# A message-passing layer on one core: tiles of 125 edges, the resident columns copied by VectorE instead of ScalarE, and silu made by ScalarE

## The chip, the cores and the metric

The kernel runs on one core of one Trainium2 chip. The time is device microseconds of one execution; the time before is the median of three runs. A profile is one more execution, taken with the hardware profiler; its own time and its span stand in the table below. Engines are named as in the profile: PE is TensorE, PEld its weight loads, DVE is VectorE, ACT is ScalarE, POOL is GpSimd, SP is SyncE. L513 is line 513 of the kernel before.

## The reference

12500 nodes have 64 features, 412500 edges 32 features each, sorted by receiver. All is float32.

```python
h = maximum(layernorm(x), 0)
msg_in = concatenate([h[src], h[dst], edge_attr], -1)          # 412500 x 160
messages = silu(msg_in @ W1 + b1) @ W2 + b2                    # 64 wide
att = softmax(silu(msg_in @ Wa1 + ba1) @ Wa2 + ba2, axis=0)    # over all edges
agg = segment_sum(messages * att, dst, 12500)
out = x + silu(concatenate([h, agg], -1) @ Wu1 + bu1) @ Wu2 + bu2
```

## The kernel before

**Node stage** (L132 to L279). Nodes lie 98 to a partition. The layer norm is made in chunks; hT, the transposed h, stays in SBUF (64 features of a node in one half of the partitions, so two nodes share a column). Two tables go to DRAM, each 128 floats a node: ts_d is h times the sender's part of Wa1 and W1 (`senders`, L226), tr_d the receiver's part with the bias (L267 to L278). The weights are halved beforehand (L248), so that the sum of an edge is half of the pre-activation.

**Edge loop** (`one_pass`, L360). Edges are taken in tiles of EP = 128, eight tiles (K) to a group: 403 groups (NG). The loop at L718 runs over the groups; every engine's program order is fixed by `pin`, so the order of the calls is the order of the work:

- `load(g+2)` (L504): eight indirect DMAs of GpSimd (L513), one for each tile, each fetching 128 rows of 512 bytes of ts_d, by the senders' numbers, into a tile gs of a pool with 7 buffers. SP fetches the window of tr_d that the group's receivers lie in (wins, L534), the edges' features (eo) and the receivers' numbers (dbs) for four groups at a time. DVE makes the one-hot rows of the receivers (L538). PE multiplies: one-hot and edge features by window and edge weights, into the PSUM tile pe (L542).
- Every second group from group 8 on is *chosen*: its last tile isn't gathered. Instead ScalarE copies one column of hT for each of its 128 edges, four bytes on each partition, at an address in a register (`columns`, L483). The registers are loaded 32 at a time (L479), in four bursts that are spread over two groups (`burst`, L486, SLOTS). DVE zeroes the half of the column that belongs to the other node (L547) and PE multiplies by the sender's weights (L548).
- `begin(g)` (L550): DVE adds gathered rows and PSUM into gs (L553; a chosen tile is copied, L555); ScalarE takes the tanh (L556).
- `end(g)` (L558): DVE makes silu from tanh, (tanh + 1) times the half sum, for the messages (L566, into acts) and for the attention (L572), multiplies by Wa2 (L574) and sums to one logit an edge (L577).
- Batches of four groups share a running maximum: `top` (L585), `weigh` (L599), which takes exp on ScalarE (L610) after the maximum over partitions.
- `sum_up` for a group some five earlier: `by_node` (L614) makes on DVE, with eight operations of 40 elements (L620), matrices that hold an edge's weight in its receiver's column; PE sums the messages with them (L626); ScalarE copies the result (L632), PE projects it (L637), and `put` (L640) adds it to the resident sums (L651, L655) and notes the maximum that they stand for (L658).

**Tail** (L789 on): the sums are rescaled, and the update of the nodes is made in 13 tiles.

If a receiver lies outside its window, a general path (L285) is run instead; it isn't with these inputs.

Of the kernel before, what the change touches and what calls it, by code (L numbers as in the profile page):

```python
# [19 lines left out]
EP = 128  # L20
# [37 lines left out]
def gnn_kernel(ctx: ExitStack, tc: tile.TileContext, n_edges, x, src, src_row, dst, dst_row, first, edge,  # L58
# [73 lines left out]
    with tc.tile_pool(name="node1", bufs=1) as node1, \  # L132
# [3 lines left out]

        sizes = [8] + [min(CB, NB - 16 - c) for c in range(0, NB - 16, CB)] + [8] if NB > 16 else [NB]
# [38 lines left out]
        pin(nc.scalar.activation(node1.tile([P, 1], F32, name="spare"), eps, AF.Sqrt))  # L176
        xms, sqs, rstds, hs, tss = ({} for _ in range(5))
# [5 lines left out]
        def subtract(i):  # L183

            n = chunks[i][1]
            total = node.tile([P, CB], F32, name="total")[:, :n]
            pin(nc.vector.tensor_reduce(total, xcs[i], AX.X, ALU.add))
            xm = xms[i] = node.tile([P, CB, D], F32, name="xm", bufs=3)[:, :n, :]
            pin(nc.vector.scalar_tensor_tensor(xm, total[:, :, None].to_broadcast([P, n, D]), -1.0 / D,
                                               xcs[i], op0=ALU.mult, op1=ALU.add))  # L190

        def square(i):
            n = chunks[i][1]
            sq = sqs[i] = node.tile([P, CB, D], F32, name="sq", bufs=3)[:, :n, :]
            pin(nc.scalar.activation(sq, xms[i], AF.Square))

        def totals(i):
            n = chunks[i][1]
            rstd = rstds[i] = node.tile([P, CB], F32, name="rstd")[:, :n]
            pin(nc.vector.tensor_reduce(rstd, sqs.pop(i), AX.X, ALU.add))  # L200
# [4 lines left out]
        def normal(i):  # L205
            n = chunks[i][1]
            rstd = rstds.pop(i)
            pin(nc.vector.reciprocal(rstd, rstd))
# [35 lines left out]
        nch = len(chunks)  # L244
# [22 lines left out]
        for c, nn in chunks:  # L267
# [9 lines left out]
            pin(nc.sync.dma_start(  # L277
                tr_d[:NP, :].rearrange("(p b) f -> p b f", b=NB)[:, c:c + nn, :], tr))  # L278
        pin(nc.sync.dma_start(tr_d[NP:, :], zero[:WR, :]))  # L279
# [80 lines left out]
def one_pass(tc, n_edges, v):  # L360
# [17 lines left out]
    with ExitStack() as ctx:  # L378
# [43 lines left out]
        with tc.tile_pool(name="work2", bufs=2) as work2, \  # L422
                tc.tile_pool(name="small", bufs=3) as small, \
                tc.tile_pool(name="pre_ps", bufs=AHEAD + 1, space=PSUM) as pre_ps, \
                tc.tile_pool(name="one_ps", bufs=1, space=PSUM) as one_ps:
            pes, gss, lgs, ps_, psums, sps, pps, ees, mts, nums, cols = ({} for _ in range(11))
# [12 lines left out]
            chosen = {g: i for i, g in enumerate(picks)}  # L439
            hT8 = v["hT"].rearrange("d b p -> d (b p)").bitcast(U8)  # L440
            sets = [(i, min(P, len(picks) - i)) for i in range(0, len(picks), P)]
# [3 lines left out]
            def places():  # L445
# [4 lines left out]
                for k, (i, n) in enumerate(sets):  # L450
                    e = (picks[i] * K + K - 1) * EP
                    nc.sync.dma_start(num[:n, k, :], bass.AP(
                        tensor=v["src_row"].tensor, offset=v["src_row"][:, e:].offset,
                        ap=[[EVERY * K * EP, n], [1, EP]]))
# [8 lines left out]
                for k, (i, n) in enumerate(sets):  # L463
                    nc.sync.dma_start(par_d[k * P:k * P + n, :], low[:n, k, :])
# [3 lines left out]
            def numbers(g):  # L468
                if g in chosen:
                    n = nums[g] = small.tile([P, EP], I32, name="half", bufs=3)  # L470
                    row = par_d[chosen[g]:chosen[g] + 1, :]
                    nc.sync.dma_start(n, bass.AP(tensor=row.tensor, offset=row.offset, ap=[[0, P], [1, EP]]))
                    cols[g] = small.tile([P, EP], F32, name="cols", bufs=3)

            def columns(g, first, n):
                if g not in chosen:
                    return
                to, i = cols[g].bitcast(U8), chosen[g]
                _, regs = nc.values_load_multi_w_load_instructions(  # L479
                    spots[i % P:i % P + 1, i // P, first:first + n], engines=[ENG.Activation],  # L480
                    min_val=HT_AT, max_val=HT_AT + 2 * NP - 4, skip_runtime_bounds_check_because=WHY)
                for i in range(n):
                    pin(nc.scalar.copy(to[:, 4 * (first + i):4 * (first + i) + 4],  # L483
                                       hT8[:, bass.ds(regs[i] - HT_AT, 4)]))

            def burst(g, k):  # L486
# [6 lines left out]
            tr_w = bass.AP(tensor=tr_d.tensor, offset=tr_d.offset,  # L493
                           ap=[[C, NP + WR - SHIFT], [SHIFT * C, 2], [1, C]])

            def registers(g, engine, at, base=base_sb, top=NP - 1):
                n = min(NQ, NG + (base is not base_sb) - g)
# [6 lines left out]
            def load(g):  # L504

                t = g * K
                if g % NQ == 0:
                    registers(g, ENG.SP, at_sp)
                full = gather.tile([P, K, C], F32, name="gs")
                gs = gss[g] = full[:EP]  # L510
                for j in range(K - (g in chosen)):
# [21 lines left out]
                for r in range(2):  # L533
                    nc.sync.dma_start(win[r * R:(r + 1) * R, :, r, :],  # L534
                                      tr_w[bass.ds(at_sp[g], R), :, :])
# [14 lines left out]
            def begin(g):  # L550

                n = K - (g in chosen)
                pin(nc.vector.tensor_tensor(gss[g][:, :n, :], pes[g][:, :n, :], gss[g][:, :n, :], ALU.add))  # L553
                if n < K:
                    pin(nc.vector.tensor_copy(gss[g][:, n, :], pes[g][:, n, :]))  # L555
                pin(nc.scalar.activation(pes[g], gss[g], AF.Tanh))  # L556

            def end(g, then=None):  # L558

                s = batch[g]  # L560
                if g == starts[s]:
                    lgs[s] = small.tile([EP, B * K], F32, name="lg")
                gs, th = gss.pop(g), pes.pop(g)

                def message():
                    pin(nc.vector.scalar_tensor_tensor(acts[g % ACTS][:, :, 0:U], th[:, :, U:C], 1.0,  # L566
                                                       gs[:, :, U:C], op0=ALU.add, op1=ALU.mult))

                if g < NG - 1:
                    message()  # L570
                att = th[:, :, 0:U]
                pin(nc.vector.scalar_tensor_tensor(att, th[:, :, 0:U], 1.0, gs[:, :, 0:U],  # L572
                                                   op0=ALU.add, op1=ALU.mult))
# [3 lines left out]
                pin(nc.vector.tensor_reduce(lgs[s][:, k:k + K], att, AX.X, ALU.add))  # L577
# [4 lines left out]
                if g == NG - 1:  # L582
                    message()

            def top(s):  # L585

                n = size[s] * K
                lg = lgs[s]
# [10 lines left out]
            def weigh(s):  # L599
# [5 lines left out]
                fall = small.tile([P, 1], F32, name="fall")  # L605
                pin(nc.vector.tensor_tensor(fall, nmax[:, s + 1:s + 2], nmax[:, s:s + 1], ALU.subtract))
                pin(nc.scalar.activation(scale[:, s:s + 1], fall, AF.Exp))
                p = ps_[s] = small.tile([EP, B * K], F32, name="p")
                psum = small.tile([EP, 1], F32, name="psum")
                pin(nc.scalar.activation(p[:, :n], lgs.pop(s)[:, :n], AF.Exp, bias=nmax[:EP, s + 1:s + 2],  # L610
                                         accum_out=psum))
                psums[s] = psum

            def by_node(g):  # L614
# [4 lines left out]
                for j in range(K):  # L619
                    pin(nc.vector.tensor_scalar(wt[:, j, :], iota_w[:EP, j // H, :],  # L620
                                                dloc[:, g * K + j:g * K + j + 1],
                                                p[:, k + j:k + j + 1],
                                                op0=ALU.is_equal, op1=ALU.mult))
# [94 lines left out]
            for g in range(NG):  # L718
# [6 lines left out]
                begin(g)  # L725
                if more and g < NG - 1:
# [10 lines left out]
                if g + AHEAD < NG:  # L737
                    load(g + AHEAD)
                numbers(g + 6)
# [384 lines left out]
```

## Time and profile before

| | |
|---|---|
| median of 3 runs | 3902.49 us (3900.42 to 3908.46) |
| profiled execution | 3904.89 us, span 3903.1 us |
| granted TensorE clock, mean | 0.642 |
| instructions | 72226 |
| indirect DMAs of POOL | 3032, busy 2871.4 us |
| column copies of ACT | 24576, busy 2415.5 us |
| DMA traffic | 391.30 MB, mean 100 GB/s |

How to read it: the page gives each engine's busy time, then groups of instructions by line, engine, operation and tile: busy time in all, mean length of one, then the engine's idle time before them and what ended it. "issue" is idle time that ended with nothing the profile shows, such as work of the engine's own sequencer. A time line gives start, length and, in brackets, the idle time ahead. Lengths of instructions that follow each other closely overlap, so what one takes of its engine is the distance of two starts.

### The profile page before, as it was taken

The page shows a single profiled execution, that of the slowest core. Times are in us where ns is not written, and L with a number is a line of the kernel's source. Part 1 is how long each engine was busy: PE and PEld are TensorE (multiplying, and loading weights), DVE is VectorE, ACT ScalarE, POOL GpSimd, SP SyncE. Part 2 cuts the span into 40 slices and gives each one's busy share as a digit, 9 for nine tenths or more (in the row PEclk, how much of TensorE's full clock was granted, in tenths as well). Part 3 has the DMA queues.
Part 4 walks back from the last instruction along what each step waited for, and adds up shares of the span by engine and source line. Part 5 has one row for each costly group of instructions (what it writes and reads, how often), then busy time and mean ns, then how long its engine had stood idle before and what let it go on. Part 6 is the DMA issues. An engine that isn't in the chain of part 4 may idle for free. (4 is left out here: it accounts for less than half of the span.)

```text
span 3903.1 us, 72226 instructions
## 1 busy us (share of the span) xinstructions
PE 2368.6 (61%) x11368; PEld 1927.2 (49%) x11368; DVE 3115.4 (80%) x8929; ACT 2954.1 (76%) x25797; POOL 2888.6 (74%) x3057
## 2 busy tenths in 40 slices
PE   6566656666666666665665656556565565555655
PEld 5454444454445554554444545445444454444545
DVE  6888787878788888887877877778777777877887
ACT  2887777777778888887877777878877878878712
POOL 3777777777777777777777777777777777777774
PEclk8766566666666657666666666666666666666666
DMA  7433334333433333333333333333333333333343
GB/s 280 114 104 94 102 100 106 94 104 99 107 93 97 97 97 91 94 97 94 87 97 85 97 93 89 97 86 97 93 88 97 86 96 91 90 97 86 95 116 86
DMA packets 228304, 391.30 MB, mean 100 GB/s; under 512 B 72369, under 2 KB 155762, under 8 KB 214770
## 3 DMA queue, kind: packets, MB, share of 16 engines
q0 software_dynamic: 97024, 198.90, 19.5%
q1 hardware_dynamic: 130802, 187.73, 17.9%
q14 instruction: 385, 3.15, 0.3%
q8 instruction: 93, 1.52, 0.2%
HBM read 360.52 MB, written 25.82 MB: 99 GB/s over the span
## 5 line engine op out<-in xcount | busy, mean ns | idle before, releaser
L513 POOL DMA_INDIRECT gs<-ts_d,src_sb x3032 | 2871.4, 947 | 973.1 <-issue 844.2
L483 ACT COPY cols<-hT 128x4 uint8 x24576 | 2415.5, 189 | 595.2 <-issue 594.2
L542 PE MATMUL pe<-wins,eo 128*128 128x256 f32 x3224 | 1470.7, 630 | 846.4 <-DVE eo L538 619.9
L542 PEld LDWEIGHTS pe<-wins,eo 128*128 128x128 f32 x3224 | 964.4, 316 | 1145.4 <-DVE eo L538 708.6
L620 DVE TENSOR_SCALAR wt<-iota_w,dloc,p 128x40 f32<-128x40 f32 x3224 | 726.9, 323 | 1.8
L553 DVE TENSOR_TENSOR gs<-pe,gs 128x1024 f32<-128x1024 f32 (+1 forms) x403 | 467.0, 1159 | 325.7 <-DMA gs<-ts_d,src_sb 303.3
L626 PE MATMUL sp<-wt,acts 128*65 128x40 f32 x6448 | 621.9, 268 | 4.6 <-DVE wt L620 3.5
L626 PEld LDWEIGHTS sp<-wt,acts 128*65 128x65 f32 x6448 | 586.0, 183 | 11.4 <-DVE wt L620 6.2
L556 ACT ACTIVATE pe<-gs 128x1024 f32<-128x1024 f32 x403 | 410.6, 1019 | 215.9 <-DVE gs L553 125.3
L637 PEld LDWEIGHTS mt<-ss,w2u 65*128 65x128 f32 x806 | 201.7, 281 | 330.4 <-issue 291.9
L637 PE MATMUL mt<-ss,w2u 65*128 65x40 f32 x806 | 183.7, 322 | 255.5 <-DVE gm L603 221.4
L566 DVE SCALAR_TENSOR_TENSOR acts<-pe,gs 128x512 f32<-128x512 f32 x403 | 277.6, 689 | 21.6 <-ACT pe L556 12.2
L574 DVE TENSOR_TENSOR pe<-pe,w_all 128x512 f32<-128x512 f32 x403 | 281.8, 699 | 13.5
L572 DVE SCALAR_TENSOR_TENSOR pe<-pe,gs 128x512 f32<-128x512 f32 x403 | 280.3, 696 | 10.5
L596 PE MATMUL mt<-ident,mx 128*128 128x128 f32 x107 | 46.7, 437 | 396.4 <-DVE sums L655 375.9
L577 DVE TENSOR_REDUCE lg<-pe 128x8 f32<-128x512 f32 x403 | 276.7, 687 | 10.5
L538 DVE TENSOR_SCALAR eo<-dbs,bj 64x256 f32<-64x256 int32 x806 | 275.5, 371 | 9.2
L596 PEld LDWEIGHTS mt<-ident,mx 128*128 128x128 f32 x107 | 19.2, 179 | 408.3 <-issue 404.5
L658 DVE COPY stand<-nmax 64x40 f32 x806 | 159.0, 197 | 3.4 <-issue 0.3
L547 DVE SCALAR_TENSOR_TENSOR cols<-half,cols 128x128 f32<-128x128 int32 x192 | 67.1, 349 | 100.6 <-ACT cols L483 98.5
L651 DVE SCALAR_TENSOR_TENSOR sums<-sums,scale,mt 64x40 f32 x214 | 54.4, 254 | 110.9 <-PE mt L637 107.4
L548 PEld LDWEIGHTS pe<-stack,cols 128*128 128x128 f32 x384 | 121.7, 317 | 32.5
(126 smaller groups left out, 957.6 us busy)
## 6 DMA issues: line engine op xcount, KB each, us to landing
eo<-in_edge_dram SPq DMA_DIRECT2D x100, 512.0 KB
dbs<-in_dst_row_dram SPq DMA_DIRECT2D x200, 256.0 KB
gs<-ts_d,src_sb POOLq DMA_INDIRECT x3032
wins<-tr_d SPq DMA_DIRECT2D x806, 32.0 KB
half<-par_d SPq DMA_DIRECT2D x192, 64.0 KB
ts_d<-ts SPq DMA_DIRECT2D x5, 896.0 KB
tr_d<-tr SPq DMA_DIRECT2D x5, 896.0 KB
hT_d<-hT SPq DMA_DIRECT2D x7, 448.0 KB
```

The costliest lines, as they stand in the source:

```text
L483: pin(nc.scalar.copy(to[:, 4 * (first + i):4 * (first + i) + 4], hT8[:, bass.ds(regs[i] - HT_AT, 4)]))
L513: nc.gpsimd.indirect_dma_start(out=full[:rows, j, :], out_offset=None, in_=ts_d[:, :], in_offset=bass.IndirectOffsetOnAxis(ap=src_full[:ro ...
L542: pin(nc.tensor.matmul(pe[:, 2 * q:2 * q + 2, :], eo[:, q * EP:(q + 1) * EP], win[:, q // 2, :, :], start=True, stop=q < H - 1 or g not in ...
L553: pin(nc.vector.tensor_tensor(gss[g][:, :n, :], pes[g][:, :n, :], gss[g][:, :n, :], ALU.add))
L556: pin(nc.scalar.activation(pes[g], gss[g], AF.Tanh))
L566: pin(nc.vector.scalar_tensor_tensor(acts[g % ACTS][:, :, 0:U], th[:, :, U:C], 1.0, gs[:, :, U:C], op0=ALU.add, op1=ALU.mult))
L572: pin(nc.vector.scalar_tensor_tensor(att, th[:, :, 0:U], 1.0, gs[:, :, 0:U], op0=ALU.add, op1=ALU.mult))
L574: pin(nc.vector.tensor_tensor(att, att, wa2[:EP, None, :].to_broadcast([EP, K, U]), ALU.mult))
L577: pin(nc.vector.tensor_reduce(lgs[s][:, k:k + K], att, AX.X, ALU.add))
L620: pin(nc.vector.tensor_scalar(wt[:, j, :], iota_w[:EP, j // H, :], dloc[:, g * K + j:g * K + j + 1], p[:, k + j:k + j + 1], op0=ALU.is_equ ...
L626: pin(nc.tensor.matmul(sp, acts[g % ACTS][:, j, :], wt[:, j, :], start=j == 0, stop=j == K - 1))
L637: pin(nc.tensor.matmul(pp, w2u.rearrange("s h u -> s (h u)"), sps.pop(g), start=True, stop=True))
```

## The change

EP goes from 128 to 125 (413 groups for 403), and every gather fetches 125 rows (WIDE = 125). PHASE = 9 leaves no group chosen for ScalarE. ROW0 = 1000 leaves nothing to a new helper that would have SP fetch rows one by one. Instead the groups g from 9 to 400 with g % 8 in (1, 4, 6) are chosen for VectorE (147 of them), whose column copies are spread evenly over all groups from 4 on: registers are loaded in two portions of 23 or 24 a group (`vcolumns`), and the copies are put where DVE would wait (`spare_columns`): before the logits, behind them, and between the steps of `weigh`.

ScalarE makes silu itself, in two activations from PSUM, and the two DVE operations that made it from tanh go. The add of `begin` now writes to PSUM, and gs is free again after it. exp is replaced: t = tanh of a 32nd of the exponent, (1 + t)/(1 - t), squared four times, on DVE but for the last square. `by_node` makes its matrices with two operations of 320 elements. The first four groups (FILL) aren't gathered from ts_d: at the start POOL fetches rows of x for their edges, and the node stage normalises and multiplies them along with the last table. SP's window reads take byte addresses that DVE has multiplied beforehand.

```diff
-EP = 128
+EP = 125
-PHASE = 0
+PHASE = 9
+FILL = 4
-WIDE = 128
+WIDE = 125
+ROW0 = 1000
+VTURN = 8
+VRES = (1, 4, 6)
+VSTART = 4
+VLATER = 5
+VBUFS = 3
...
+        early = node1.tile([P, FILL * K], I32, name="early")
+        nc.sync.dma_start(early, src[:, :FILL * K])
+        for g in range(FILL):
+            for j in range(K):
+                nc.gpsimd.indirect_dma_start(
+                    out=xes[g][:, j, :], out_offset=None, in_=x[:, :],
+                    in_offset=bass.IndirectOffsetOnAxis(ap=early[:, g * K + j:g * K + j + 1], axis=0))
...
+            vpicks = [g for g in range(VSTART + VLATER, NG - 12) if g % VTURN in VRES]
...
+            def vcolumns(g, part):
+                at, end = (i * EP * len(VRES) // (2 * VTURN) for i in (2 * (g - VSTART) + part,
+                                                                        2 * (g - VSTART) + part + 1))
+                end = min(end, len(vpicks) * EP)
+                while 0 <= at < end:
+                    t, first = vpicks[at // EP], at % EP
+                    n = min(end - at, EP - first)
+                    if first == 0:
+                        cols[t] = small.tile([P, EP], F32, name="vcols", bufs=VBUFS)
+                    loads, regs = spots_of(t, first, n, ENG.DVE)
+                    for one in loads:
+                        pin(one)
+                    to = cols[t].bitcast(U8)
+                    waiting.extend((to[:, 4 * (first + i):4 * (first + i) + 4], regs[i]) for i in range(n))
+                    at += n
+
+            def spare_columns(n=None):
+                for to, reg in waiting[:n]:
+                    pin(nc.vector.tensor_copy(to, hT8[:, bass.ds(reg - HT_AT, 4)]))
+                waiting[:] = waiting[len(waiting) if n is None else n:]
...
-                for j in range(K - (g in chosen)):
+                for j in range(K - (g in chosen) - (g in fetched) if g >= FILL else 0):
...
-                pin(nc.vector.tensor_tensor(gss[g][:, :n, :], pes[g][:, :n, :], gss[g][:, :n, :], ALU.add))
-                if n < K:
-                    pin(nc.vector.tensor_copy(gss[g][:, n, :], pes[g][:, n, :]))
-                pin(nc.scalar.activation(pes[g], gss[g], AF.Tanh))
+                pin(nc.vector.tensor_tensor(pe[:, :n, :], pe[:, :n, :], gs[:, :n, :], ALU.add))
...
+                att = atts[g] = silus.tile([P, K, U], F32, name="att")[:EP]
+                pin(nc.scalar.activation(att, pe[:, :, 0:U], AF.Silu, scale=2.0))
+                pin(nc.scalar.activation(acts[g % ACTS][:, :, 0:U], pe[:, :, U:C], AF.Silu, scale=2.0))
...
-                pin(nc.scalar.activation(p[:, :n], lgs.pop(s)[:, :n], AF.Exp, bias=nmax[:EP, s + 1:s + 2],
-                                         accum_out=psum))
+                pin(nc.scalar.activation(t, lg[:, :n + 1], AF.Tanh, bias=part, scale=1.0 / 32))
+                spare_columns()
+                pin(nc.vector.tensor_scalar(d, t, -1.0, 1.0, op0=ALU.mult, op1=ALU.add))
+                spare_columns(3)
+                pin(nc.vector.reciprocal(d, d))
+                spare_columns(3)
+                pin(nc.vector.scalar_tensor_tensor(t, t, 1.0, d, op0=ALU.add, op1=ALU.mult))
+                for _ in range(3):
+                    spare_columns(3)
+                    pin(nc.vector.tensor_tensor(t, t, t, ALU.mult))
+                pin(nc.scalar.activation(p[:, :n], t[:EP, :n], AF.Square, accum_out=psum))
...
-                for j in range(K):
-                    pin(nc.vector.tensor_scalar(wt[:, j, :], iota_w[:EP, j // H, :],
-                                                dloc[:, g * K + j:g * K + j + 1],
-                                                p[:, k + j:k + j + 1],
-                                                op0=ALU.is_equal, op1=ALU.mult))
+                at = dloc[:, g * K:(g + 1) * K].rearrange("p (r h) -> p r h", h=H)
+                pin(nc.vector.tensor_tensor(wt.rearrange("p (r h) w -> p r h w", h=H),
+                                            iota_w[:EP, :, None, :].to_broadcast([EP, 2, H, W]),
+                                            at[:, :, :, None].to_broadcast([EP, 2, H, W]), ALU.is_equal))
+                pin(nc.vector.tensor_tensor(wt, wt, p[:, k:k + K, None].to_broadcast([EP, K, W]), ALU.mult))
...
                 begin(g)
+                vcolumns(g, 0)
...
+                spare_columns()
+                vcolumns(g, 1)
                 end(g)
...
                     weigh_upto(batch[g] - 1)
+                spare_columns()
```

More of the change, by code (lines that the diff above doesn't have):

```diff
@@ L242, in senders, with filled @@
                     ts_d.rearrange("(p b) f -> p b f", b=NB)[:, c:c + nn, :], tss.pop(i)))
-        nch = len(chunks)
+        ready = []
+        def filled(i):
+            h = hs.pop(i)
+            pt = node_ps.tile([P, 4, P], F32, name="pt")
+            for k in range(K // 2):
+                pin(nc.tensor.transpose(pt[:, k, :], h[:, 2 * k:2 * k + 2, :], ident))
+            he = node.tile([2 * D, K // 2, P], F32, name="he")
+            pin(nc.scalar.copy(he, pt))
+            gs = gather.tile([P, K, C], F32, name="gs")
+            for b in range(0, K, 4):
+                pn = node_ps.tile([P, 4, C], F32, name="pn", bufs=4)
+                for k in range(0, 4, 2):
+                    pin(nc.tensor.matmul(pn[:, k:k + 2, :], he[:, (b + k) // 2, :],
+                                         w_pair[:, 0], start=True, stop=True))
+                pin(nc.scalar.copy(gs[:, b:b + 4, :], pn))
+            ready.append(gs)
         squares(0)
@@ L278, in gnn_kernel @@
                 tr_d[:NP, :].rearrange("(p b) f -> p b f", b=NB)[:, c:c + nn, :], tr))
+        squares(nch)
+        for i in range(FILL):
+            totals(nch + i)
+            deviation(nch + i)
+            if i + 1 < FILL:
+                subtract(nch + i + 1)
+                square(nch + i + 1)
+            if i > 0:
+                filled(nch + i - 1)
+            for c in chunks[i * nch // FILL:(i + 1) * nch // FILL]:
+                receivers(*c)
+            normal(nch + i)
+        filled(nch + FILL - 1)
         pin(nc.sync.dma_start(tr_d[NP:, :], zero[:WR, :]))
@@ L425, in one_pass @@
                 tc.tile_pool(name="one_ps", bufs=1, space=PSUM) as one_ps:
-            pes, gss, lgs, ps_, psums, sps, pps, ees, mts, nums, cols = ({} for _ in range(11))
+            pes, gss, atts, lgs, ps_, psums, sps, pps, ees, mts, nums, cols = ({} for _ in range(12))
             w2t_ps = one_ps.tile([P, 4, P], F32, name="mt")[:U, 0, :S1]
@@ L488, in burst @@
                     columns(g + 3 + i, *SLOTS[EVERY - 1 - i][k])
-            at_sp, at_lo, at_hi, bus, rest = {}, {}, {}, {}, {}
[L493 to L497, printed above, removed]
+            fetched = {}
+            for i in range(NG):
+                g = ROW0 + (EP * (i + 1) - 1) // ROWS + 2
+                if g < NG - 12:
+                    fetched[g] = i
@@ new lines, in fetch @@
+            def fetch(g):
+                at = (g - ROW0) * ROWS
+                end = min(at + ROWS, len(order) * EP)
+                if g == ROW0 - 3:
+                    ask(0)
+                if g == ROW0 - 2:
+                    scaled(0)
+                while 0 <= at < end:
+                    i, first = at // EP, at % EP
+                    n = min(end - at, EP - first)
+                    if first < ROWS:
+                        ask(i + 1)
+                    if EP // 2 <= first < EP // 2 + ROWS:
+                        scaled(i + 1)
+                    if first == 0:
+                        lone[order[i]] = small.tile([P, C], F32, name="lone", bufs=2)
+                    to = lone[order[i]]
+                    loads, regs = nc.values_load_multi_w_load_instructions(
+                        ids[i][0:1, first:first + n], engines=[ENG.SP], min_val=0, max_val=(NP - 1) * 4 * C,
+                        skip_runtime_bounds_check_because=WHY)
+                    for one in loads:
+                        pin(one)
+                    for k in range(n):
+                        pin(nc.sync.dma_start(to[first + k:first + k + 1, :].bitcast(U8),
+                                          ts8[bass.ds(regs[k], 4 * C)][None, :]))
+                    at += n
@@ new lines, in one_pass, with registers @@
+            at_sp, at_lo, at_hi, bus, rest = {}, {}, {}, {}, {}
+            row = 4 * C
+            tr8 = tr_d.bitcast(U8)
+            tr_w = bass.AP(tensor=tr8.tensor, offset=tr8.offset,
+                           ap=[[1, (NP - 1) * row + 1], [row, R], [SHIFT * row, 2], [1, row]])
+            base_by = keep.tile([1, NG + 1], I32, name="base_by")
+            nc.vector.tensor_scalar(base_by[:, :NG], base_sb[:, :NG], 9, None, op0=ALU.logical_shift_left)
+            def registers(g, engine, at, base, top):
+                n = min(NQ, NG + (base is not base_by) - g)
@@ L561, in end @@
                 if g == starts[s]:
[L562 to L573, printed above, removed]
+                    lgs[s] = small.tile([P, B * K + 1], F32, name="lg")
+                    if EP < P:
+                        pin(nc.vector.memset(lgs[s][P - R:], 0.0))
+                att = atts.pop(g)
                 pin(nc.vector.tensor_tensor(att, att, wa2[:EP, None, :].to_broadcast([EP, K, U]),
```

98 lines of the change are left out of this document (65 added, 33 removed).

## The prediction

> **What bounds the kernel now.** I read the page's busy times first, then its costliest groups, then the time lines of GpSimd (POOL), VectorE (DVE) and ScalarE (ACT) in the middle of the run and at both ends. The page:
>
> ```profile
> PE 2368.6 (61%) x11368; PEld 1927.2 (49%) x11368; DVE 3115.4 (80%) x8929; ACT 2954.1 (76%) x25797; POOL 2888.6 (74%) x3057
> L513 POOL DMA_INDIRECT gs<-ts_d,src_sb x3032 | 2871.4, 947 | 973.1 <-issue 844.2
> L483 ACT COPY cols<-hT 128x4 uint8 x24576 | 2415.5, 189 | 595.2 <-issue 594.2
> ```
>
> No engine looks full. But POOL's idle time is "issue": it waits for nothing that the profile shows. Its time line, first and last gathers and two of the middle:
>
> ```profile
> 51.68 1.10 POOL L513 DMA_INDIRECT gs<-ts_d,src_sb  x1 [49.29 <-DMA ts_d<-ts]
> ...
> 2003.39 0.95 POOL L513 DMA_INDIRECT gs<-ts_d,src_sb  x1 [0.30 <-issue]
> 2004.64 0.95 POOL L513 DMA_INDIRECT gs<-ts_d,src_sb  x1 [0.30 <-issue]
> ...
> 3845.97 0.94 POOL L513 DMA_INDIRECT gs<-ts_d,src_sb  x1 [0.30 <-issue]
> ```
>
> 3032 gathers start between 51.68 and 3845.97: (3845.97 - 51.68)/3031 = 1.252 us each, 0.95 busy and 0.30 of issue, with no gap. The gather stream is the bound; 7.52 gathers a group make 9.4 us a group. DVE confirms it: in the list of waits its largest is for the gathers. PE's largest is for DVE's eo.
>
> ```profile
> PE pe L542 <- DVE eo L538: 619.9, 258, 7.3
> ...
> DVE gs L553 <- DMA gs<-ts_d,src_sb: 303.3, 225, 3.9
> ```
>
> What DVE does in a group is read from its time line; columns are start, length, and in brackets the idle time before:
>
> ```profile
> 2001.21 1.09 DVE L553 TENSOR_TENSOR gs<-pe,gs 128x896 f32<-128x896 f32 x1 [1.02 <-DMA gs<-ts_d,src_sb]
> 2002.22 0.28 DVE L555 COPY gs<-pe 128x128 f32<-128x128 f32 x1
> 2002.42 0.18 DVE L655 TENSOR_TENSOR sums<-sums,mt 64x40 f32 x1
> 2002.52 0.17 DVE L658 COPY stand<-nmax 64x40 f32 x1
> ...
> 2003.12 0.61 DVE L538 TENSOR_SCALAR eo<-dbs,bj 64x256 f32<-64x256 int32 x2
> ...
> 2003.91 1.78 DVE L620 TENSOR_SCALAR wt<-iota_w,dloc,p 128x40 f32<-128x40 f32 x8
> ...
> 2011.40 1.23 DVE L553 TENSOR_TENSOR gs<-pe,gs 128x1024 f32<-128x1024 f32 x1 [0.98 <-DMA gs<-ts_d,src_sb]
> 2012.55 0.34 DVE L538 TENSOR_SCALAR eo<-dbs,bj 64x256 f32<-64x256 int32 x1
> 2012.80 1.76 DVE L620 TENSOR_SCALAR wt<-iota_w,dloc,p 128x40 f32<-128x40 f32 x8
> 2014.48 0.68 DVE L566 SCALAR_TENSOR_TENSOR acts<-pe,gs 128x512 f32<-128x512 f32 x1
> 2015.20 0.70 DVE L572 SCALAR_TENSOR_TENSOR pe<-pe,gs 128x512 f32<-128x512 f32 x1
> 2015.93 0.70 DVE L574 TENSOR_TENSOR pe<-pe,w_all 128x512 f32<-128x512 f32 x1
> 2016.66 0.69 DVE L577 TENSOR_REDUCE lg<-pe 128x8 f32<-128x512 f32 x1
> ```
>
> The starts give what an instruction really takes of DVE: add 1.01 or 1.15, put 0.70, both eo 0.50, eight wt 1.68, the four 512-element operations 0.7 each.
>
> **The change, part by part.** *Tiles of 125 edges.* 412500/1000 gives 413 groups for 403. Gathers: 413 x 8 = 3304, less 147 columns picked (groups 9 to 400 with remainder 1, 4 or 6 of 8), so 3157; of these, 32 fetch rows of x for groups 0 to 3 while POOL waits for ts_d (it did nothing until 51.68; 32 x 1.25 is 40), so 3125 remain against 3032. In steady state 7.625 a group. No row shows a gather of 125 rows. By rows it would cost 0.947 x 125/128 + 0.305 = 1.23, unchanged 1.252; I take 1.252, the nearest row, and keep cheaper gathers as a rival. POOL then needs 7.625 x 1.252 = 9.55 us a group.
>
> *The start.* The four filled groups hold four of the seven gather buffers; groups 4 to 6 take the rest, and POOL then waits until group 0's add frees one. So the stream hangs on that add, which was here:
>
> ```profile
> 96.40 1.23 DVE L553 TENSOR_TENSOR gs<-pe,gs 128x1024 f32<-128x1024 f32 x1 [2.96 <-PE pe L542]
> ...
> 102.85 1.22 DVE L553 TENSOR_TENSOR gs<-pe,gs 128x1024 f32<-128x1024 f32 x1
> ```
>
> The fills add five operations of 0.2 to 0.7 each, 2.9 us, per group to DVE's prologue, partly under its waits there: 11.7 at most, I take 8, so the first add is at 104.
>
> *What ScalarE loses* (all 24576 column copies) gains nothing, since nothing waits long for it. Two silus take the place of one tanh and lie under DVE's other work:
>
> ```profile
> 2003.47 1.02 ACT L556 ACTIVATE pe<-gs 128x1024 f32<-128x1024 f32 x1
> ```
>
> The first half of that (some 0.6) must be done before the logits, over 4 us of DVE work later; if that cover were gone it would cost those 0.6.
>
> *What DVE loses and gains.* Gone: L555, L566 and L572 (1.5 us a group). The eight wt become two operations of 320 elements. From L574 (512 elements, 0.70) and L606 (one element, 0.16) 320 take 0.50; the second waits for the first: 0.95 in place of 1.68. Per batch of four groups, exp leaves and a chain of some eight small operations and a reciprocal of 33 comes in:
>
> ```profile
> L606 DVE TENSOR_TENSOR fall<-nmax 128x1 f32<-128x1 f32 x107 | 17.0, 159 | 3.7
> L208 DVE RECIPROCAL rstd<-rstd 128x14 f32<-128x14 f32 (+2 forms) x8 | 1.8, 227 | 5.0 <-ACT rstd L203 4.9
> ```
>
> 8 x 0.2 + 0.4 with 1.0 that is there already: 3.0 a batch, 0.76 a group. Without columns a group costs DVE: add 1.10 (five of eight at 1.15, three at 1.01) + put 0.70 + eo 0.50 + column mask 0.13 + wt 0.95 + logits 1.40 + batch 0.76 = 5.54 us. Output to PSUM in the add is taken at the same price.
>
> *The columns on DVE* are 147 x 125 = 18375 copies of four bytes, 46.9 a group. The trace has none on DVE. Bounds: ScalarE's own, 32 in 3.14 us, so 0.095 each; and DVE's L655, whose successor starts 0.10 later with 40 elements, 36 more than a column, at (0.70 - 0.16)/511 = 1.06 ns an element: 0.06. A column is nearest to the latter: 0.07, so 3.28 us a group (2.8 to 4.5).
>
> Each half group also loads 23.4 addresses into registers of the issuing engine, and meanwhile it issues nothing:
>
> ```profile
> 2004.89 3.14 ACT L483 COPY cols<-hT 128x4 uint8 x32 [0.28 <-issue]
> 2008.96 0.19 ACT L483 COPY cols<-hT 128x4 uint8 x1 [0.93 <-issue]
> ...
> L479 ACTq TENSOR_LOAD <-spots x768: 1942/2008/2800, 98.4 to 3706.6; - x192
> ...
> L498 DVEq TENSOR_LOAD <-bases x202: 336/343/600, 142.4 to 3853.0; - x101
> ```
>
> On ScalarE 32 addresses take 2.0 us, of which 0.93 is bare behind queued copies. On DVE four take 0.34. By ScalarE's row 23.4 take 1.46. The first load stands behind the add (1.1 us of cover), the second behind 23 copies, of which the queue covers what it covered on ScalarE, some eleven copies (0.77). Bare: 0.4 + 0.7; I take 1.0 a group. Behind the first load stand put, eo and wt, and PE waits for eo; behind the second the logits, which only the batch's maximum needs. Ends: nothing, if further addresses are as cheap as the first four suggest, and 2.9 if none is covered.
>
> So DVE: 5.54 + 3.28 + 1.0 = 9.8 us a group, over POOL's 9.55. **DVE becomes the bound.** The same method gives 7.4 for before, where DVE's 3115.4 over 403 groups is 7.7 with prologue and tail.
>
> *Rest.* PE keeps its matmuls; SP's window reads change their address form, not their bytes; both have slack. The batch chain's new wait for ScalarE's tanh has 23 copies ahead of it (1.6 us) and costs nothing while copies are left; behind it on DVE stands the next add, so without them it would cost some 0.5 a batch.
>
> [...] The new copies read and write SBUF with one input. The gather of 2004.64 lies under the eight tensor_scalars of 2003.91 and takes 0.95 where the mean is 0.947. [...]
>
> [...]
>
> **The sum.** First add at 104; four groups without columns at 5.5: 22; 392 groups at 9.8: 3842; the last 17, no columns left but POOL with eight gathers a group and six groups of lead: 115; from the last add (3849.81) to the end 53:
>
> ```profile
> 3849.81 1.23 DVE L553 TENSOR_TENSOR gs<-pe,gs 128x1024 f32<-128x1024 f32 x1 [1.64 <-DMA gs<-ts_d,src_sb]
> ```
>
> 104 + 22 + 3842 + 115 + 53 = 4136 of span. Before has 3903.1 of span in a run of 3904.9; that run is 2.4 over the median of 3902.5. So 4136 + 1.8 - 2.4 = **4135 us**.
>
> **Rivals.** *A, the forecast*: 4135. 43%.
>
> *B, the gathers stay the bound*: loads are covered or copies come at 0.06. POOL: 104 + (406 groups x 8 - 147 = 3101) x 1.252 + 57 after the last gather's start = 4044; 3966 at 1.23. For it: DVE is within 3% of POOL. 20%.
>
> *C, faster*: a gather of 125 rows is built more cheaply than one of 128. Now:
>
> ```profile
> q0 software_dynamic: 97024, 198.90, 19.5%
> ```
>
> That is 32 packets a gather, sixteen of data and sixteen others if data come in 4 KB. [...] It decides from a pitch below (3903 - 161)/3101 = 1.207, and only if DVE takes less than (3903 - 294)/392 = 9.2, that is, with covered loads. Then DVE at 8.82 gives 104 + 22 + 3457 + 100 + 53 = 3736; between, up to 3895. [...] 20%.
>
> *D, much slower*: copies at ScalarE's 0.095 make DVE 5.54 + 4.45 + 1.0 = 11.0 and the run 4606; loads bare as well, 12.9 and 5350. [...] Together 15%. The last 2% are no change.
>
> **Numbers.** The range 3780 to 4620 takes in A and B with their bounds, the slower half of C and the near end of D; about 2 in 10 lie outside. 0.2% (8 us) is about what a measurement of this kernel tells from no change. Faster 20%, same 2%, slower 78%.
>
> **What would show it.** A: no idle of POOL's issue alone; it waits for DVE's add, and DVE has over 90% busy or idles by "issue" before the columns. B: POOL at 1.25 without gaps, DVE waiting for gathers. C: mean gather well under 947 ns. D: column pitch over 0.09, or gathers that grow beside columns. The forecast is wrong if loads of 24 addresses are short or if the gather's price depends on its rows.

## The result, and the profile after

The changed kernel takes **6913 us** in the median of four runs (6907 to 6918), before 3902 us beside it (3900 to 3908): 1.771 times as long, 95% interval 1.768 to 1.774. The forecast was 4135, its range 3780 to 4620. The profiled execution has a span of 6905.2 us.

The page of after, busy times, two DMA and GpSimd rows, and the groups of VectorE that matter (busy, mean ns, then idle before them and what ended it):

```profile
PE 2462.9 (36%) x11589; PEld 2015.3 (29%) x11589; DVE 3857.4 (56%) x24982; ACT 616.9 (9%) x1684; POOL 3841.5 (56%) x3182
...
q0 software_dynamic: 251024, 204.69, 13.2%
...
L649 POOL DMA_INDIRECT gs<-ts_d,src_sb x3125 | 3787.7, 1212 | 3008.9 <-DVE pe L690 2133.2
...
L568 DVE COPY vcols<-hT 128x4 uint8 x18375 | 1432.0, 204 | 147.7 <-issue 147.5
L706 DVE TENSOR_TENSOR att<-att,w_all 125x512 f32<-125x512 f32 x413 | 286.1, 693 | 1065.9 <-issue 1061.6
L798 DVE TENSOR_TENSOR sums<-sums,mt 64x40 f32 x606 | 117.5, 194 | 1041.3 <-issue 1036.0
...
L704 DVE MEMSET lg<- 32x33 f32 x110 | 9.5, 86 | 473.9 <-issue 473.3
```

Again no engine is full. GpSimd now waits 2133 us for VectorE's add (L690), which frees its buffers. VectorE works 56% of the span; before L706, L798, L704 and L568 it idles 2718 us by "issue", 6.9 us for each of the 392 groups with columns. The list of waits says the same from the others' side:

```profile
PE pe L678 <- DVE eo L674: 2674.0, 344, 14.9
POOL gs L649 <- DVE pe L690: 2133.2, 384, 13.7
DVE att L706 <- issue: 1061.6, 296, 5.4
DVE sums L798 <- issue: 1036.0, 288, 4.9
```

One group on VectorE's time line (start, length, in brackets the idle before):

```profile
3503.96 1.10 DVE L690 TENSOR_TENSOR pe<-pe,gs 125x896 f32<-125x896 f32 x1
3509.78 0.19 DVE L798 TENSOR_TENSOR sums<-sums,mt 64x40 f32 x1 [4.72 <-issue]
...
3512.35 2.12 DVE L568 COPY vcols<-hT 128x4 uint8 x23
3519.07 0.69 DVE L706 TENSOR_TENSOR att<-att,w_all 125x512 f32<-125x512 f32 x1 [4.60 <-issue]
...
3520.40 1.79 DVE L568 COPY vcols<-hT 128x4 uint8 x24
3522.22 1.23 DVE L690 TENSOR_TENSOR pe<-pe,gs 125x1024 f32<-125x1024 f32 x1
```

Two holes of 4.7 and 4.6 us, one behind the add, one behind the copies: the places of the two register loads. VectorE's sequencer in the same trace, all loads of column addresses, min/median/max in ns:

```profile
L535 DVEq TENSOR_LOAD <-spots x882: 1601/4490/5906, 131.6 to 6712.9; - x177
```

The 882 loads sum to 3427 us, 8.7 a group. Sorted by address they fall into two heaps. The tile of addresses is [128, 3, 125] words, so portion `first` of set k begins at word 125k + first. Where that is a multiple of four (a multiple of 16 bytes; 245 loads, all of 23 or 24 registers), 24 registers take 1.67 us and 23 take 2.12. Where it is not (637 loads), 24 take 5.60, 23 take 5.36, 16 take 3.70, 8 take 1.90: some 0.235 us for each register.

From 1000 to 6000 us a group takes 16.72 us on VectorE: some 9.59 of work (3.68 for the columns, 5.91 for the rest; short gaps are counted with the work) and 7.13 of bare time, in which it idles, nearly all of it by "issue".

### The profile page after: what moved, and what is told of

Same layout as the page of the kernel before. It is cut to its first block, busy times and chain, and to the rows that moved or that the text cites. A ratio compares the mean times of both kernels' runs of the same rounds, so it can differ in the third digit from the quotient of the medians.

```text
span 6905.2 us, 62474 instructions
## 1 busy us (share of the span) xinstructions
PE 2462.9 (36%) x11589; PEld 2015.3 (29%) x11589; DVE 3857.4 (56%) x24982; ACT 616.9 (9%) x1684; POOL 3841.5 (56%) x3182
## 3 DMA queue, kind: packets, MB, share of 16 engines
q0 software_dynamic: 251024, 204.69, 13.2%
## 5 line engine op out<-in xcount | busy, mean ns | idle before, releaser
L649 POOL DMA_INDIRECT gs<-ts_d,src_sb x3125 | 3787.7, 1212 | 3008.9 <-DVE pe L690 2133.2
L678 PE MATMUL pe<-wins,eo 128*125 128x256 f32 x3304 | 1523.6, 640 | 2731.9 <-DVE eo L674 2674.0
L678 PEld LDWEIGHTS pe<-wins,eo 128*125 128x125 f32 x3304 | 1018.0, 323 | 3032.6 <-DVE eo L674 2744.3
L568 DVE COPY vcols<-hT 128x4 uint8 x18375 | 1432.0, 204 | 147.7 <-issue 147.5
L706 DVE TENSOR_TENSOR att<-att,w_all 125x512 f32<-125x512 f32 x413 | 286.1, 693 | 1065.9 <-issue 1061.6
L798 DVE TENSOR_TENSOR sums<-sums,mt 64x40 f32 x606 | 117.5, 194 | 1041.3 <-issue 1036.0
L769 PE MATMUL sp<-wt,acts 125*65 125x40 f32 x6608 | 659.6, 275 | 27.3 <-DVE wt L766 27.2
L769 PEld LDWEIGHTS sp<-wt,acts 125*65 125x65 f32 x6608 | 628.2, 193 | 31.8 <-DVE wt L766 31.5
L690 DVE TENSOR_TENSOR pe<-pe,gs 125x1024 f32<-125x1024 f32 (+1 forms) x413 | 488.1, 1182 | 32.3 <-issue 12.0
L674 DVE TENSOR_SCALAR eo<-dbs,bj 64x250 f32<-64x250 int32 x826 | 284.8, 385 | 18.8 <-issue 8.8
L709 DVE TENSOR_REDUCE lg<-att 125x8 f32<-125x512 f32 x413 | 281.8, 682 | 11.0
L704 DVE MEMSET lg<- 32x33 f32 x110 | 9.5, 86 | 473.9 <-issue 473.3
L766 DVE TENSOR_TENSOR wt<-wt,p 125x320 f32<-125x320 f32 x413 | 204.5, 495 | 14.2
L801 DVE COPY stand<-nmax 64x40 f32 x826 | 190.4, 231 | 3.0 <-issue 2.0
```

The source lines that it names most:

```text
L568: pin(nc.vector.tensor_copy(to, hT8[:, bass.ds(reg - HT_AT, 4)]))
L649: nc.gpsimd.indirect_dma_start(out=full[:rows, j, :], out_offset=None, in_=ts_d[:, :], in_offset=bass.IndirectOffsetOnAxis(ap=src_full[:ro ...
L674: pin(nc.vector.tensor_scalar(eo[:WR, e], db[:, e], bj[g // NQ % 2 * WR:(g // NQ % 2 + 1) * WR, g, h:h + 1], None, op0=ALU.is_equal))
L678: pin(nc.tensor.matmul(pe[:, 2 * q:2 * q + 2, :], eo[:, q * EP:(q + 1) * EP], win[:, q // 2, :, :], start=True, stop=q < H - 1 or g not in ...
L690: pin(nc.vector.tensor_tensor(pe[:, :n, :], pe[:, :n, :], gs[:, :n, :], ALU.add))
L706: pin(nc.vector.tensor_tensor(att, att, wa2[:EP, None, :].to_broadcast([EP, K, U]), ALU.mult))
```

## The experiments

Theory 1: **a load of registers from an address that is no multiple of 16 bytes fetches them one by one, and VectorE issues nothing meanwhile.** Rival 2: columns and gathers hold one another up. Rival 3: the dearer gather sets the time. The experiments e1 to e6 and e12 are one run each; the others are four.

**e1, aligned loads.** Every portion is 24 addresses (fewer at a tile's end) from a multiple of 8; the tiles keep 125 edges.

```diff
-            spots = keep.tile([P, len(sets), EP], I32, name="spots")
+            spots = keep.tile([P, len(sets), P], I32, name="spots")
...
-                at, end = (i * EP * len(VRES) // (2 * VTURN) for i in (2 * (g - VSTART) + part,
+                at, end = (i * P * len(VRES) // (2 * VTURN) for i in (2 * (g - VSTART) + part,
```

> The changed kernel with only the place of the column addresses moved: each tile's 125 addresses start on a row of 128, and every half group takes 24 of them from a multiple of 8, so that every register load starts on a 16-byte boundary. Copies, gathers (125 rows) and everything else stay. Theory 1 (loads that start off a 16-byte boundary fetch one register at a time, 0.235 us each, and VectorE issues nothing meanwhile): loads of 24 fall from 3.9 us on average to 1.66, VectorE's bare time from 7.1 to some 1.4 us a group, its group from 16.7 to 11.0; GpSimd then needs 7.625 x 1.51 = 11.5, becomes the bound without gaps, and the time is 115 + 3101 x 1.51 + 57 = 4855 us (4700 to 5000). [...] Rival 3 (the dearer gather of 125 rows sets the time): unchanged, about 6900.

Measured 4987 us, 1926 less, within the theory's range. Both rivals said 6900. Loads and GpSimd's group in e1:

```profile
L535 DVEq TENSOR_LOAD <-spots x882: 593/1644/2392, 133.9 to 4731.6; - x177
```

```profile
L650 POOL DMA_INDIRECT gs<-ts_d,src_sb x3125 | 3834.8, 1227 | 1042.0 <-issue 895.0 <-DVE pe L691 67.4 <-DVE near L517 29.4
```

The same 882 loads, median 1.64 for 4.49. GpSimd now waits for nearly nothing but its own issue. It and VectorE are both nearly full: an add starts 74 us behind the end of its group's last gather at 800 us, and 3 us behind it from 4000 us on. So GpSimd falls back slowly, and with 125 rows it becomes the bound late in the run.

**e2, aligned loads and 128 rows** (`rows = P` in every gather).

> As the aligned loads, and every gather fetches 128 rows in place of 125 (three more rows of the table that nothing reads). Theory 1: the gather returns to 1.252 us each, GpSimd needs 9.55 us a group, and VectorE with 9.6 us of work and some 1.4 of bare loads is the bound at 11.0: 115 + 22 + 392 x 11.0 + 115 + 54 = 4620 us (4400 to 4750). If loads were fully covered it would be 9.6 a group and 4070. Rival 2: about 6900. Rival 3: 6913 less 3125 x (1.51 - 1.252) = 806, so 6100.

Measured 4776, a little over the range: VectorE needs 11.24 a group, 9.51 of work and 1.72 bare.

```profile
L650 POOL DMA_INDIRECT gs<-ts_d,src_sb x3125 | 3002.9, 961 | 1643.6 <-issue 798.3 <-DVE pe L691 753.1 <-DVE near L517 35.3
```

The gather is back at 961 ns and waits for VectorE again.

**e3, 128 rows alone.**

> The changed kernel with only its gathers widened from 125 to 128 rows; loads stay where they were. Theory 1: GpSimd waits for VectorE in any case, so the time stays at 6910 within 1%, with more idle on GpSimd. Rival 3: 6100. [...]

Measured 6822: 91 us less where theory 1 had nothing (1% at most), far from rival 3's 806 and from the some hundreds that rival 2 would give. The rows place those 91 us on VectorE: its column copies are busy 1394.7 us in place of 1432.0, its copies of stand (L801) 170.6 in place of 190.4, and its idle by "issue" at the four lines is 2685 in place of 2718. So a little of rival 2 is there; why these are shorter beside shorter gathers was not tried.

**e4, tiles of 128 edges** (`EP = WIDE = 128`).

> The changed kernel with tiles of 128 edges again: 403 groups, portions of exactly 24 addresses on rows of 128 (aligned without any padding) and gathers of 128 rows; the columns stay on VectorE, three tiles in eight groups. Theory 1: the cure of both at once, 115 + 22 + 382 x 11.1 + 110 + 54 = 4540 us (4250 to 4650), slower than before by VectorE's work alone. Rivals 2 and 3: still over 6000.

Measured 4675, again a little over: aligned and with 128 rows, the change still loses 20% to before, by VectorE's work and what is left bare of its loads (1.6 of 11.25 us a group).

**e5 and e12, the mirror of e1.** As e4, with every portion moved by one word:

```diff
-            spots = keep.tile([P, len(sets), EP], I32, name="spots")
+            spots = keep.tile([P, len(sets), P + 4], I32, name="spots")[:, :, 1:P + 1]
```

> Tiles of 128 edges as before in this series (4675 us), with one thing changed: the tile of column addresses begins one word later in its partition, so that every portion of 24 starts 4 bytes past a 16-byte boundary. Same instructions, same portions, same gathers. Theory 1 (a register load off a 16-byte boundary goes register by register): each load 24 x 0.235 = 5.6 us in place of 1.65, two a group 11.3 for 3.3, the cover unchanged, so 382 x 8.0 = 3050 us more: 7700 (7400 to 7900), slower even than the changed kernel. Rival (what the aligned runs gained came from portions of equal size, or from rows of 128): 4675 within 2%.

> The shifted column addresses at tiles of 128 edges, once more beside an undisturbed kernel before: VectorE's idle before column copies was 505 us there against 119 in the unshifted run. Theory 1: without those 390 us, 7340 (7250 to 7500); the loads themselves 11.0 us a group against 3.3, as there. Rival (equal portions or padded rows were the cure): 4675.

Measured 7727 and 7701. One word costs some 3050 us, with instructions and portions unchanged. Loads in e4, then in e5, then in e6, which has e4's aligned loads and ran on e5's chip:

```profile
L535 DVEq TENSOR_LOAD <-spots x864: 592/1610/1856, 132.4 to 4504.9; - x173
```

```profile
L535 DVEq TENSOR_LOAD <-spots x864: 1841/5408/5830, 170.9 to 7507.2; - x173
```

```profile
L535 DVEq TENSOR_LOAD <-spots x864: 592/1617/2871, 211.1 to 9352.6; - x173
```

The loads sum to 1261 us in e4 and to 4221 in e5, so 2960 of the 3050 us are the loads themselves. e4 ran beside a kernel before of 3903 us, e5 and e12 on chips where before itself took 5987 and 5852 (see e7 to e11). e6's row shows that aligned loads are as short on such a chip.

My 7340 for e12 was wrong: the 505 us of idle before column copies came back. In e5's trace 489 of them stand right behind a load and 16 between two copies, so they too are the loads'. Theory 1 stands; the rival had 4675.

**e6, the price of a gather by its rows.** Seven extra gathers a group, whose rows nothing reads.

> The price of a gather by its rows: tiles of 128 edges, and behind each group's own gathers seven more that fetch 127, 126, 125, 124, 120, 112 and 64 rows into a tile that nothing reads. GpSimd becomes the bound at some 19 us a group (7000 to 8500 us in all). Theory (the rows of a gather are spread over as many lists as divide them, 16 at most, and GpSimd pays more where they are few): 120 and 112 and 64 (15, 16, 16) cost no more than the 0.95 of 128, 126 (14) about as much, 125 (5) the 1.19 that it has in the changed kernel, 124 (4) and 127 (1) 1.2 or more. Rival (any number below 128 takes a slower path): 1.19 for all seven, 64 perhaps less. Second rival (by rows alone): falling from 0.95 to 0.5, which the changed kernel's 1.19 contradicts.

GpSimd's time line, one round of the seven in the order 127, 126, 125, 124, 120, 112, 64 rows:

```profile
2022.83 2.56 POOL L654 DMA_INDIRECT spare_rows<-ts_d,src_sb  x1 [0.30 <-issue]
2025.70 0.99 POOL L654 DMA_INDIRECT spare_rows<-ts_d,src_sb  x1 [0.30 <-issue]
2026.99 1.21 POOL L654 DMA_INDIRECT spare_rows<-ts_d,src_sb  x1 [0.30 <-issue]
2028.51 1.29 POOL L654 DMA_INDIRECT spare_rows<-ts_d,src_sb  x1 [0.30 <-issue]
2030.11 0.97 POOL L654 DMA_INDIRECT spare_rows<-ts_d,src_sb  x1 [0.30 <-issue]
2031.39 0.96 POOL L654 DMA_INDIRECT spare_rows<-ts_d,src_sb  x1 [0.30 <-issue]
2032.65 0.92 POOL L654 DMA_INDIRECT spare_rows<-ts_d,src_sb  x1 [0.30 <-issue]
```

The price follows the largest divisor up to 16: 2.56 for 127 rows (1), 1.29 for 124 (4), 1.21 for 125 (5), 0.99 for 126 (14), 0.97 for 120 (15), 0.92 to 0.96 for 64 and 112 (16). One step from 126 to 127 costs 1.57 us. Both rivals fall. The total, 9567, is over the 7000 to 8500 expected and says nothing of the price: the extra gathers of many groups were put ahead of those that VectorE waited for.

**e7 to e11, columns on both engines.** Tiles of 128, the even groups' columns on ScalarE (`PHASE = 0`) and two, one or none of the odd groups in eight on VectorE (`VRES = (1, 5)`, `(1,)`, `()`).

> Columns on both engines: tiles of 128 edges, ScalarE makes the columns of every even group as before the change, VectorE those of two odd groups in eight (16 addresses a half group, aligned). The theory's budget for a group: GpSimd 7.25 x 1.252 = 9.08, VectorE 5.95 + 32 x 0.078 + 0.1 + some 0.5 of bare loads = 9.05, ScalarE 7.7. GpSimd is the bound: 115 + 2877 x 1.252 + 57 = 3774 us, faster than before by 3% (3740 to 3880). Rival (engines that copy columns at the same time slow one another, or the gathers): over 3903.

> As the run with two odd groups in eight, with one odd group in eight on VectorE (8 addresses a half group). GpSimd 7.375 x 1.252 = 9.23, VectorE 7.6: 115 + 2924 x 1.252 + 57 = 3833 us (3800 to 3870). If it is faster than two in eight, VectorE was the bound there.

> The version with two odd groups in eight on VectorE and the even groups on ScalarE, once more: in the call before, the kernel before itself took 5987 us, and ScalarE idled 0.5 or 1.2 us by issue between single column copies, so that call says nothing of the budget. As there: GpSimd 7.25 x 1.252 = 9.08 us a group is the bound, VectorE 9.05, so 3774 us (3740 to 3880), faster than before by 3%. Rival: two engines that copy columns at the same time, or the gathers beside them, slow one another: over 3903.

> One odd group in eight on VectorE, once more: GpSimd 7.375 x 1.252 = 9.23, VectorE 7.6: 115 + 2924 x 1.252 + 57 = 3833 us (3800 to 3870).

> The changed kernel with tiles of 128 edges, the even groups' columns on ScalarE as before the change, and none on VectorE: what the rest of the change (silu on ScalarE, the two wide wt operations, the four filled groups) is worth alone. GpSimd 7.5 x 1.252 = 9.39 us a group stays the bound: 115 + 2972 x 1.252 + 57 = 3893 us, 0.2% under before (3870 to 3905). If VectorE's shorter work had mattered in the kernel before, it would be faster than that.

Beside e7 and e8 the kernel before took 5987 us itself, and beside e9 to e11 5852. In e8 and e11 ScalarE idles 2521 and 2272 us by issue before its column copies, mostly between single copies, where e14 below, the same kernel as e11, has 546. What holds it is open, so these times aren't compared with others. Beside that kernel before, two in eight came to 0.934 (0.931 to 0.938) and 0.953 (0.949 to 0.957), one in eight to 1.058 (1.053 to 1.063) and 1.053 (1.048 to 1.058), none to 1.059 (1.055 to 1.064).

**e13 to e15, the same beside a kernel before of 3908 us.**

> Even groups' columns on ScalarE, two odd groups in eight on VectorE, tiles of 128. If the kernel before takes its 3902 us beside it: 115 + 2877 x 1.252 + 57 = 3774 us (3740 to 3880). If it takes over 5000 as in the two calls before, ScalarE's idle by issue sets the time again, near 5580, and the budget stays untested.

> Even groups' columns on ScalarE, none on VectorE. Beside 3902: 115 + 2972 x 1.252 + 57 = 3893 us (3870 to 3905). Beside over 5000: near 6200, as in the call before.

> Even groups' columns on ScalarE, one odd group in eight on VectorE. Beside 3902: 115 + 2924 x 1.252 + 57 = 3833 us (3800 to 3870). Beside over 5000: 6150 to 6350.

Measured 4140 (1.060, 1.058 to 1.062), 4035 (1.033, 1.031 to 1.035) and 4040 (1.034, 1.032 to 1.036): all slower than before, and 4035 where the budget gave 3893. The rival of e7 named such a time (over 3903), but column copies aren't slower for being made on both engines: in e13 they start every 95 ns on ScalarE, as in before, and every 0.073 us on VectorE, as in e4. In e14 the gather's mean is 978 ns against before's 947. I sorted e14's gathers by what VectorE did meanwhile: of those that overlap L706 (att times wa2, all in SBUF) 54% take over 1.05 us, beside L766 (wt times p, all in SBUF) 35%, beside the add from PSUM, where no such product is near, 2%. In before the product L574 has an input and its output in PSUM: 1 of 514 (from 300 us on).

**e16 to e18, those products taken away.** Theory 4: VectorE's products from SBUF to SBUF hold the gathers. e16 keeps att in PSUM; e17 also makes wt with eight tensor_scalars, as before; e18 adds one odd group in eight.

```diff
-                att = atts[g] = silus.tile([P, K, U], F32, name="att")[:EP]
+                att = atts[g] = pe[:, :, 0:U]
```

> Columns on ScalarE alone (4035 us), with one change: silu's result att stays in PSUM in place of its input, so that the product with wa2 reads and writes PSUM as in the kernel before. Theory 4 (a VectorE product with both inputs and the output in SBUF holds up GpSimd's gathers): mean gather from 978 to some 955 ns, 2972 x 0.023 = 70 us less: 3965 (3930 to 3990). Rival 5 (new waits between ScalarE and VectorE make the difference): 4035 within 0.5%.

> As att in PSUM, and wt made by eight tensor_scalars as in the kernel before, in place of two products of 320 elements (0.75 us a group more on VectorE, which is not the bound). Theory 4: mean gather back to 948 ns, 115 + 2972 x 1.252 + 57 = 3893 us (3880 to 3935). Rival 5: no faster than 4035; by VectorE's 0.75 a group slower if VectorE sets the pace.

> As the run before, with one odd group in eight on VectorE (8 addresses a half group, aligned). Theory 4: GpSimd 7.375 x 1.252 = 9.23 us a group, VectorE 5.9 + 0.75 + 1.3 + some 0.3 of loads = 8.3: 115 + 2924 x 1.252 + 57 = 3833 us (3815 to 3880), faster than the kernel before by 2%. Rival 5: near the 4040 of the version without the two edits.

The gathers of e14, e16 and e17:

```profile
L649 POOL DMA_INDIRECT gs<-ts_d,src_sb x3000 | 2935.1, 978 | 970.8 <-issue 798.6 <-DVE pe L690 64.2 <-DMA gs<-ts_d,src_sb 19.2
```

```profile
L649 POOL DMA_INDIRECT gs<-ts_d,src_sb x3000 | 2882.8, 961 | 1408.9 <-issue 859.3 <-DVE pe L690 492.6 <-DVE eo L674 34.1
```

```profile
L649 POOL DMA_INDIRECT gs<-ts_d,src_sb x3000 | 2837.8, 946 | 1474.3 <-issue 853.1 <-DVE pe L690 500.4 <-DVE sums L798 59.2
```

The gathers shorten as theory 4 has it: 978, 961, 946 ns, and in e17 one of 2829 takes over 1.05 us. That is 97 us of GpSimd's time, but the runs' times went the other way: 4421 (1.133, 1.131 to 1.135), 4460 (1.143, 1.141 to 1.145) and 4474 (1.147, 1.145 to 1.148). All three expected times missed, rival 5's 4035 too, because VectorE's adds hardly waited for the gathers in any version from e13 on. From 1600 to 3600 us an add of the kernel before starts 2.2 us behind the end of its group's last gather. In e13, e14 and e15 it starts 56, 52 and 52 us behind, in e16 to e18 61 to 63, so the rows lie ready long before, though in e14 GpSimd itself has hardly a gap but its issue. In that stretch e13, e14 and e15 also take the same 9.6 us a group, with 7.25, 7.5 and 7.375 gathers. What VectorE waits for in e14 is ScalarE, and hardly the gathers, its largest wait in before:

```profile
DVE cols L683 <- ACT cols L545: 560.0, 167, 4.0
DVE d L742 <- ACT t L740: 520.1, 104, 5.7
DVE att L706 <- ACT att L695: 219.5, 97, 3.2
...
DVE pe L690 <- DMA gs<-ts_d,src_sb: 29.9, 100, 0.6
```

And e16's edit lengthens ScalarE's part. ScalarE's idle before its columns, in e14 and then in e16:

```profile
ACT cols L545 <- issue: 545.8, 757, 1.7
```

```profile
ACT cols L545 <- issue: 919.8, 767, 1.7
```

Silu in place ties its two activations together on one tile, and ScalarE's loads of 32 addresses lie where fewer queued copies cover them: 374 us more, next to the 386 that e16 lost. That is read from the rows, not tried. So e14's 142 us over the budget are not the gathers': the budget took the wrong bound. That ScalarE and VectorE set the pace by waiting for each other is read from the waits; no run took one of these waits away. Beside a kernel before of 3902 to 3908 us no version here beats it.

## Why the prediction was wrong, point by point

- **The direction and the bound: right.** VectorE became the bound, and idles "by issue", as the forecast's own test had it, though before L706 and L798 more than before the columns.
- **The step that failed: "Bare: 0.4 + 0.7; I take 1.0 a group", from "By ScalarE's row 23.4 take 1.46".** It measured 7.13. ScalarE's loads of 32 began at multiples of 32 words and VectorE's of four at multiples of four: both rows were aligned, and so was the far end of 2.9. The tile of 125 words and portions of 23 and 24 were in the diff; 637 of 882 loads start off the boundary. 392 x (7.13 - 1.0) = 2403 of the 2769 us between the forecast's span and the measured one. e1 and e5 show it from both sides.
- **VectorE's work: a little small.** 5.91 in place of 5.54 a group (among others the add at 1.18, both eo at 0.67) is 145 us; columns 3.68 in place of 3.28 another 157. In a run of copies the pitch is 0.071, as taken; the mean with the first and last of each run is 0.079.
- **The gather of 125 rows: "I take 1.252, the nearest row".** Measured 1.50 (1.20 busy, 0.30 issue):

```profile
3507.11 1.18 POOL L649 DMA_INDIRECT gs<-ts_d,src_sb  x1 [0.30 <-issue]
3508.60 1.20 POOL L649 DMA_INDIRECT gs<-ts_d,src_sb  x1 [0.31 <-issue]
```

  In the changed kernel VectorE's delay covers it. In e1 GpSimd is full with it, and e2 is 211 us shorter without it. **Rival C had the sign wrong**: a gather of 125 rows is dearer for GpSimd than one of 128 (1.20 us busy for 0.947), not cheaper. e6's prices go by the largest divisor up to 16, size by size. The packets go by it too: a gather of 128 rows has sixteen of 4096 bytes in before, and one of 125 has fifteen of 4096 and five of 512 in after, as five equal portions of 25 rows would give (the lists of e6's expectation). e6 has 127 packets of 512 bytes and more over e4's for each of its 399 rounds of seven, which is what 1, 14, 5, 4, 15, 16 and 16 portions give if each is split at 4096 bytes. That 125 rows would be cheaper was my estimate, and the runs showed the opposite: q0's 251024 packets are 80 a gather in place of 32, as 60 small ones of 4 or 32 bytes come in place of sixteen. Whether these are the price was not tried.
- **The start:** first add at 115.1, not 104.
- **Rival D's gathers that grow: hardly beside the columns, but beside an operation that I passed over.** Beside column copies 3% of e4's gathers are slow, and 1 in 1273 where no product is near. Beside products with both inputs in SBUF they are longer (54% over 1.05 us beside L706 in e14), by 31 ns in the mean of e14 (978 for 947), which cost e14 nothing that its trace shows, as its gathers lie ready 52 us ahead. The row that I weighed, eight tensor_scalars with a gather of 0.95 under them, has one SBUF tensor as input. What makes a gather longer beside such a product is not shown; e16 and e17 show that it is short again without them (961 and 946).
- **Rival B** (its 3966 at 1.23 should read 3975: 104 + 3101 x 1.23 + 57) needed covered loads and 1.252, and had neither. With both sizes cured (e2) VectorE still needs 11.24 a group, not 9.8.

## What to carry to other kernels

Before a loop that loads runs of addresses into registers, work out each run's start modulo 16 bytes: here one word moved the kernel by some 3050 us. A duration from these traces held for its alignment (24 registers in 1.67 or 5.60 us) and its divisors as well as its size; ask whether the new shape keeps them. When a tile shrinks from 128 to a number with small divisors, price the gathers again: here 125 rows took 1.21 us and 127 took 2.56, where 128 took 0.95. Before a stream of transfers is taken as the bound of a new version, see how far it runs ahead of its reader there: 2 us in before, 52 in e14.

## What the runs showed of the hardware

- Register loads on VectorE: 24 in 1.67 us from a multiple of 16 bytes, 5.60 from elsewhere (after), some 0.235 for each register.
- An indirect gather by GpSimd: 0.92 to 0.99 us for 64 to 126 rows with 14 to 16 as largest divisor, 1.21 with 5, 1.29 with 4, 2.56 with 1.
- A VectorE product from SBUF to SBUF lengthens gathers beside it (54% over 1.05 us beside L706, 978 ns in the mean of all in e14); with att's product from and to PSUM and wt made by tensor_scalars they take 946 (e17).
